# Unequal routing groups, shorter one-hot tiles, softmax by tanh and an earlier turn in a fused RNN and MoE kernel

## The chip, the cores and the metric

The kernel runs on one core of a Trainium2 chip. The metric is the device time of one execution in microseconds (us), the median over several executions. In this text PE is the matrix engine (TensorE), PEld its weight loads, DVE the vector engine, ACT the scalar engine, POOL the GpSimd engine and SP the engine that issues most DMAs. L721 is line 721 of the kernel before.

## What is computed

```python
# x (2, 1024, 256) as rows of 16 tokens; h0 = cond_1024 (2, 256)
step:   h = tanh(x_t @ Wx + b + h_prev @ Wh)          # a recurrence over 1024 tokens, two sequences
logits = h @ gate_w.T                                  # 8 experts
top_v, top_i = top_k(logits, 2)
probs  = softmax(top_v)
out    = x + sum over the two chosen experts e of
             probs_e * ((silu(h @ wg_e.T) * (h @ wu_e.T)) @ wd_e.T)   # 256 -> 1024 -> 256
```

The 2048 tokens form 16 tiles of 128. A step of the kernel's recurrence computes one tile: all 64 chunks of both sequences advance at once, and steps 48 to 63 give the tiles 0 to 15 of h that are used.

## The kernel before

**Stages.** Steps 8 to 63 of the recurrence (loop at L616, matmuls L623, tanh on ACT) come first. Routing lies among steps 49 to 63 and the first expert steps. Then the experts: the 2048 x 2 choices are sorted by expert into slots of 128 tokens; the tokens of a slot are gathered from DRAM (`rows_d`), turned into columns (`transpose_tokens`, L203), multiplied, and added to the output with an indirect DMA (`scatter`, L467). All matmuls of the experts split their operands into a high and a low part (`xhi`, `xlo`; `hh`, `hl`) and add three products.

**Routing.** Tiles are handled in groups of four (`GRP`, L36; `groups`, L341). For each tile `route_tile` (L350) transposes the tile and computes its logits on PE (L357), and ACT copies the row of 264 (256 of h, 8 logits) into the group's `rows`. `route_max` finds the two largest logits on DVE. For a group, `route_choice` makes one-hot choices `oh`, their sum `sel` and the difference `dl` of the two logits; `route_exp` takes exp(dl) on ACT; `route_position` (L388) counts on PE, by matmuls with `sel`, at which place of its expert each token stands, in `pos_ps`; `route_code` (L401) turns that into a slot number `v` and a place `m` in it, and, by `route_rows` (L446), the softmax weights, which POOL puts into `rows`; `rows_out` writes `rows` to DRAM in three DMAs on SP. `route_onehot` (L425) makes three tiles of 128 x 1024 f16 on DVE for a group: a one-hot of `v` (part 0, tile `bv`), its product with the token number (part 1), a one-hot of `m` (part 2, tile `am`). `route_slots` (L440) multiplies them on PE (L444) into `inv_ps`: for every place and slot the token that stands there.

**Early and late.** After two groups `early_slots` (L473) gathers two slots of expert 0 (POOL, L461), which hold only tokens of the first eight tiles; `early_turn` (L484) transposes them. This is unit 0. After the last group `all_slots` (L487) computes the index `gidx` and gathers the other two slots of expert 0 (unit 1). SP also writes a row `landed` that waits for the early gather (L480); what SP issues next waits behind it. `expert_order` (L496) then sorts the experts by load, in five parts.

**Order.** It is written out by hand, and every engine keeps it. `at(step, f)` (L548) notes a call under a number, `run(step)` (L551) makes all calls noted up to that number, in order of the numbers. In the recurrence `run(s - 0.5)` stands between the two halves of step s, `run(s)` behind it. An expert step n has `front` (L830: 12 matmuls of gate and up), `gate` (L849: Silu on ACT, product `g` on DVE, cast `hh` on ACT, difference on DVE) and `back` (L868: the down product) of an earlier step, with `run(64 + n + ...)` between them (L946 to L980). Unit 0's gates of steps 0 and 1 both come in step 1 (`shut`), and its `back` lags behind by two steps from step 5 on.

**Tables.** ACT holds one set of function tables at a time. Tanh and exp are in the one loaded at the start; another is loaded for Silu ahead of unit 0 (L592).

`route_max`, `route_choice`, `rows_out`, the gathers and scatters, and the split of the next expert's weights (`piece`, L766) are as before apart from their place. DVE, ACT and POOL instructions go through a helper and all have L54 in the profile, so they are told apart by their tiles.

Of the kernel before, what the change touches and what calls it, by code (L numbers as in the profile page):

```python
# [8 lines left out]
F32 = mybir.dt.float32  # L9
# [26 lines left out]
GRP = 4  # L36
# [21 lines left out]
def rnn_moe(ctx, tc, xT, xrows, h0T, Wx, Wh, b, gw, W, out):  # L58
# [21 lines left out]
    iota16 = cst.tile([P, P], F16, name="iota16")  # L80
    trash = cst.tile([P, E * SPE // MT, MT], F32, name="trash").rearrange("p a b -> p (a b)")
# [11 lines left out]
    def constants(part):  # L93
        if part == 0:
            vec.tensor_copy(iota_f, iota_i)
            vec.tensor_copy(tokp1, part_i)
            vec.tensor_scalar(ident, iota_f, 1.0, tokp1[:, 0:1], ALU.add, ALU.is_equal)
        elif part == 1:
            vec.tensor_scalar(upper, iota_f, 1.0, tokp1[:, 0:1], ALU.add, ALU.is_gt)
            vec.tensor_copy(ig[:, 0, 0:P], ident)  # L100
            vec.tensor_copy(ig[:, 1, E : P + E], ident)
            vec.tensor_copy(iota16, iota_f)
            vec.tensor_copy(tok16, tokp1.unsqueeze(2).to_broadcast([P, R, 2]))
        elif part == 2:
            vec.tensor_copy(trash, trash_i.rearrange("p a b -> p (a b)"))
            vec.memset(ones16, 1.0)
            vec.tensor_scalar(base, iota_f[:, 0:E], float(SPE), None, ALU.mult)
        else:

            vec.tensor_scalar(keyc, iota_f[:, 0:E], FIRST - 0.5, 2.0**17, ALU.is_lt, ALU.mult)  # L110
            vec.scalar_tensor_tensor(keyc, iota_f[:, 0:E], float(8 * P * SPE + 1), keyc, ALU.mult, ALU.add)
# [110 lines left out]
    rows2 = ov.tile([P, GRP * ROW], F32, name="rows2")  # L222
# [15 lines left out]
    act.activation(warm, zl[:, 0:1], AF.Tanh)  # L238
# [27 lines left out]
    pos_ps = y_tile(0)[:, 0 : (GRP + 1) * E].rearrange("p (i e) -> p i e", e=E)  # L266
# [75 lines left out]
    for g in range(R // GRP):  # L342
        o = (g % 2) * 4 * GRP * P
        gr = {"r0": g * GRP, "n": GRP}
        space = rows2 if g == 2 else xs[g % 3 % 2][:, 0 : GRP * ROW]
        gr["rows"] = space.rearrange("p (i c) -> p i c", c=ROW)
        gr["am"], gr["bv"] = (hot_space[:, o + c * 2 * GRP * P : o + (c + 1) * 2 * GRP * P].rearrange("p (i m) -> p i m", m=P) for c in range(2))
        groups.append(gr)
# [35 lines left out]
    def route_exp(gr):  # L384
        gr["ex"] = rt.tile([P, gr["n"]], F32, name="ex")
        act.activation(gr["ex"], gr["dl"], AF.Exp)

    def route_position(gr):  # L388

        n, r0 = gr["n"], gr["r0"]  # L390
        w = n + 1
        ops = [(ones16, base.unsqueeze(1).to_broadcast([P, w, E]), pos_ps), (upper, sel[:, r0 : r0 + n, :], pos_ps[:, 0:n, :])]
        for r in range(r0 + n):
            m = max(0, r - r0 + 1)
            ops.append((ones16, sel[:, r : r + 1, :].to_broadcast([P, w - m, E]), pos_ps[:, m:w, :]))
        for m, (l, x, o) in enumerate(ops):
            pe(nc.tensor.matmul(
                o.rearrange("p i e -> p (i e)"), lhsT=l, rhs=x,
                start=(m == 0), stop=(m == len(ops) - 1), skip_group_check=True))

    def route_code(gr):  # L401
        n = gr["n"]
        rows = route_rows(gr)
        tmp = rt.tile([P, n, 2, E], F32, name="tmp")
        next(rows)
        vec.tensor_tensor(tmp, gr["oh"], pos_ps[:, 0:n, :].unsqueeze(2).to_broadcast([P, n, 2, E]), ALU.mult)
        code = rt.tile([P, n, 2], F32, name="code")
        next(rows)
        vec.tensor_reduce(code, tmp, AX.X, ALU.add)
        next(rows, None)  # L410
        big = 1.5 * 2.0**23 * P
        vv = rt.tile([P, n, 2], F32, name="vv")
        vec.tensor_scalar(vv, code, 0.5 - P / 2, big, ALU.add, ALU.add)
        gr["v"] = v = rt.tile([P, 2 * n, 2], F16, name="v")
        twice = lambda t: t.rearrange("p i c -> p (i c)").unsqueeze(2).to_broadcast([P, 2 * n, 2])
        vec.tensor_scalar(v, twice(vv), -big, 1.0 / P, ALU.add, ALU.mult)
        gr["m"] = m = rt.tile([P, 2 * n, 2], F16, name="m")
        vec.scalar_tensor_tensor(m, v, -float(P), twice(code), ALU.mult, ALU.add)

    def early_gap():  # L420

        vec.tensor_scalar(gap, pos_ps[:, GRP, 0:1], -1.0 / P, float(ET), ALU.mult, ALU.add)
        vec.tensor_scalar(base[:, 0:1], gap, 0.0, None, ALU.max)

    def route_onehot(gr, part):  # L425


        n = gr["n"]
        sh = [P, 2 * n, P // 2, 2]
        pairs = lambda t: t.rearrange("p i (m t) -> p i m t", t=2)  # L430
        if part == 1:
            bv = gr["bv"].rearrange("p (i c) (m t) -> p i (c m) t", c=2, t=2)
            tok = tok16[:, gr["r0"] : gr["r0"] + n, :].unsqueeze(2).to_broadcast([P, n, P, 2])
            vec.tensor_tensor(bv, bv, tok, ALU.mult)
            return
        hot, x = ((gr["bv"], gr["v"]), None, (gr["am"], gr["m"]))[part]
        count = iota16.rearrange("p (m t) -> p m t", t=2).unsqueeze(1).to_broadcast(sh)
        vec.tensor_tensor(pairs(hot), count, x.unsqueeze(2).to_broadcast(sh), ALU.is_equal)

    def route_slots(gr, i):  # L440
        for c in range(2):
            first = gr["r0"] + i == 0 and c == 0
            last = gr["r0"] + i == R - 1 and c == 1
            pe(nc.tensor.matmul(inv_ps, lhsT=gr["am"][:, 2 * i + c, :], rhs=gr["bv"][:, 2 * i + c, :], start=first, stop=last, skip_group_check=True))  # L444

    def route_rows(gr):  # L446
        n, ex = gr["n"], gr["ex"]
        sm = rt.tile([P, n], F32, name="sm")
        vec.tensor_scalar(sm, ex, 1.0, None, ALU.add)
        yield  # L450
        pr = rt.tile([P, n, 2], F32, name="pr")
        vec.reciprocal(pr[:, :, 0], sm)
        yield
        vec.tensor_tensor(pr[:, :, 1], ex, pr[:, :, 0], ALU.mult)
# [32 lines left out]
    def all_slots():  # L487
# [4 lines left out]
        vec.scalar_tensor_tensor(key, pos_ps[:, GRP, :], 8.0, keyc, ALU.mult, ALU.subtract)  # L492
        vec.scalar_tensor_tensor(cnt, iota_f[:, 0:E], -float(P * SPE), pos_ps[:, GRP, :], ALU.mult, ALU.add)
# [72 lines left out]
    maxima.update({5: 55, 9: 59.5, 10: 60.6, 11: 61, 12: 62.2, 13: 62.3, 14: 64.05, 15: 64.06})  # L566
    for g, gr in enumerate(groups):
        for r in range(gr["r0"], gr["r0"] + gr["n"]):
            at(r + 49, route_tile, gr, r)
            at(maxima[r], route_max, gr, r)  # L570

    def group(g, choice, exp, position, code, hot, slots):
        gr = groups[g]
        at(choice, route_choice, gr)
        at(exp, route_exp, gr)
        at(choice + 0.1, rows_out, gr, ((0, P), (P + E, ROW)))
# [8 lines left out]
    group(0, 52.5, 52.6, 53.5, 53.5, (54, 54, 55), 56.5)  # L585
    group(1, 56.5, 56.6, 57.5, 57.5, (58, 58, 58), 60.1)
    at(58.1, early_gap)
    at(60.2, early_slots)
    group(2, 61, 61.1, 62, 62, (62.4, 64.1, 64.1), 65.12)
    at(63.5, early_turn)  # L590
    group(3, 64.07, 64.08, 65.1, 65.13, (65.2, 65.3, 66.3), 68.55)
    at(64.09, act.activation, warm, zl[:, 0:1], AF.Silu)  # L592
    at(68.55, all_slots)
    at(70.6, chunk_starts)
# [117 lines left out]
    with ExitStack() as c2:  # L712
# [66 lines left out]
        class Unit:  # L779
# [50 lines left out]
            def front(u, s):  # L830

                w, x = u.job.w, u.x
                if u.main:
# [8 lines left out]
                    pg, pu = (products(ab, p) for ab, p in zip(pairs, pt))  # L842
# [84 lines left out]
        def shut(n):  # L927

            u, s, j, m = step_of(n)
            low = []  # L930
            if (j, m) in split_at:
                to, p = split_at.pop((j, m))
                u.gate(s, lambda: low.append(jobs[to].piece(p, jobs[to + 1] if to + 1 < len(jobs) else None)))
            else:
                u.gate(s)
            for f in low:
                f()

        def step_of(n):
            i, s = steps[n]  # L940
            u = units[i]
            return u, s, jobs.index(u.job), s + (NIC if i and units[i - 1].job is u.job else 0)

        run(64)
        run(64.1)
        for n in range(len(steps)):  # L946
            i, s = steps[n]
            u = units[i]
            u.front(s)

            run(64 + n + 0.15)
            if n == 1:
                shut(0)
            run(64 + n + 0.2)
            if n > 0:
                shut(n)
# [7 lines left out]
            if n == 5:  # L964
                units[1].gather()
                units[2].gather()
            if i > 0 and s == 5 and i + 1 < len(units):
                units[i + 1].turn()
            for _ in range({6: 1, 7: 1, 9: 2, 11: 1}.get(n, 0)):
                next(order_ops)  # L970
            if i > 0 and s == (3 if i == 1 else 2) and i + 2 < len(units):
                units[i + 2].gather()
            if n < len(steps) - NIC + TAIL + 2:

                for late in {2: (), 3: (0,), 4: (1, 2)}.get(n, (n - 2,) if n > 4 else ()):
                    v, t = steps[late]
                    units[v].back(t)
            if n == 6:
                units[1].turn()
# [184 lines left out]
```

## Time and profile before

| | us |
|---|---|
| Median of 8 runs | 389.32 |
| Lowest and highest | 387.83, 389.66 |
| The profiled execution's own time | 389.44 |
| Its span (first to last instruction) | 387.3 |
| Steps 8 to 63 of the recurrence | to 75.3 |
| First gate matmul of unit 0 | 77.77 |
| Late gather: index, first matmul behind it | 90.55, 95.28 |
| End of PE's work | 371.9 |

A row of a timeline gives the start and the duration in us, engine, line, operation, output and inputs with their shape, the number of instructions merged, and in brackets the idle time of the engine before it and the instruction that ended it. Matmuls overlap, so that a single one looks longer than the distance to the next. In the chain of waits every step leads to what released it; its shares tell on which engine the time was spent that set the end. In a table by stages each row has the stretch, its length, busy time of PE, PEld, DVE, ACT and POOL with the number of instructions, the clock granted to PE (1.00 is full), the busy share of the DMA engines and GB/s. At its end the kernel spends some 15 us on the last scatters, from 371.9 on.

### The profile page before, as it was taken

The numbers are of one execution on the slowest core, as the hardware profiler recorded it, in microseconds if no ns is written. First come the engines' busy times: TensorE is split into PE (matmuls) and PEld (weight loads), VectorE is DVE, ScalarE is ACT, GpSimd is POOL, SyncE is SP. The second block draws the span as 40 slices with busy tenths as digits, with TensorE's granted clock in tenths as the row PEclk, the third lists the DMA queues.
The fourth block names the chain that finished last, engine by engine and source line by source line (L and its number), as shares of the span: only waits on it lengthen the run. The fifth ranks groups of instructions, "written<-read, shape, count | busy, mean of one in ns | idle before, by whom it ended". The sixth has DMA issues, their size and how long they took to land.

```text
span 387.3 us, 7243 instructions
## 1 busy us (share of the span) xinstructions
PE 370.6 (96%) x2715; PEld 350.5 (90%) x2715; DVE 227.0 (59%) x568; ACT 198.9 (51%) x460; POOL 117.7 (30%) x124
## 2 busy tenths in 40 slices
PE   8999999998999999999999999999999999999990
PEld 7998899897998889999999999999989999999890
DVE  6876648776678656574556564566545655663410
ACT  3746667543455644655446644665454555444420
POOL 3780001204264500674223602523040014006042
PEclk9999999999899999999999999999999999999996
DMA  7962334141166534665136243445143144003122
GB/s 216 414 256 96 108 111 113 31 113 46 41 162 192 154 110 136 151 195 112 68 123 130 67 130 91 85 136 137 27 111 114 47 171 53 0 2 40 12 23 35
DMA packets 19227, 42.20 MB, mean 109 GB/s; under 512 B 4802, under 2 KB 14178, under 8 KB 16066
## 3 DMA queue, kind: packets, MB, share of 16 engines
q1 hardware_dynamic: 12402, 32.32, 24.6%
q0 software_dynamic: 6496, 9.09, 14.7%
q8 instruction: 23, 0.38, 0.4%
q10 hardware_dynamic: 288, 0.26, 0.3%
q14 instruction: 18, 0.15, 0.1%
HBM read 35.15 MB, written 9.14 MB: 114 GB/s over the span
## 4 chain that ended last, share of the span: by engine, by line
PE 78%; DVE 8%; ACT 5%; POOL 3%; issue 3%; DMA 1%; POOLq 0%; DVEq 0%; ACTq 0%
PE pgu_t L721 42%; PE yb L883 21%; PE pgu_t L623 8%; PE ptr L303 2%; PE ptr L210 2%; POOL out_dram L468 2%; ACT hh L54 2%; DMA xg<-rows_d,gidx 1%; DVE wd L54 1%; DVE g L54 1%; DVE hh L54 1%; PE ptr L634 1%; ACT h L54 1%; ACT gu_g L54 1%; PE ptr L883 1%
## 5 line engine op out<-in xcount | busy, mean ns | idle before, releaser
L883 PE MATMUL yb<-wd,hh 128*128 128x256 f32 (+2 forms) x544 | 94.2, 284 | 0.2 <-ACT y L54 0.2
L54 DVE TENSOR_TENSOR g<-g,pgu_t 128x256 f32<-128x256 f32 (+5 forms) x96 | 50.1, 522 | 61.5 <-PE pgu_t L721 46.2
L883 PEld LDWEIGHTS yb<-wd,hh 128*128 128x128 f32 (+2 forms) x544 | 80.5, 185 | 2.3 <-ACT y L54 0.7
L468 POOL DMA_INDIRECT out_dram<-y,si x27 | 43.5, 1612 | 118.5 <-ACT y L54 113.0
L54 ACT CAST hh<-g 128x256 fp32r<-128x256 f32 (+5 forms) x92 | 44.6, 485 | 68.0 <-DVE g L54 67.2
L721 PE MATMUL pgu_t<-xhi,gu_g 128*128 128x256 f32 (+5 forms) x384 | 78.7, 327 | 0.3 <-ACT xhi L54 0.3
L54 ACT ACTIVATE g<-pgu_t 128x256 f32<-128x256 f32 (+5 forms) x96 | 44.8, 466 | 65.9 <-PE pgu_t L721 65.0
L721 PE MATMUL pgu_t<-xhi,gu_u 128*128 128x256 f32 (+5 forms) x384 | 78.1, 325 | 0.0
L721 PEld LDWEIGHTS pgu_t<-xhi,gu_u 128*128 128x128 f32 x384 | 61.6, 189 | 4.3
L721 PEld LDWEIGHTS pgu_t<-xhi,gu_g 128*128 128x128 f32 x384 | 59.2, 190 | 2.8 <-issue 0.5
L54 DVE TENSOR_TENSOR hl<-g,hh 128x480 fp32r<-128x480 f32 (+4 forms) x52 | 31.0, 597 | 31.8 <-ACT hh L54 31.8
L883 PE MATMUL yb<-wd,hl 128*128 128x256 f32 (+1 forms) x176 | 49.6, 282 | 0.0
L721 PE MATMUL pgu_t<-xlo,gu_u 128*128 128x256 f32 (+5 forms) x192 | 46.7, 325 | 0.0
L721 PE MATMUL pgu_t<-xlo,gu_g 128*128 128x256 f32 (+5 forms) x192 | 46.7, 324 | 0.0
L461 POOL DMA_INDIRECT xg<-rows_d,gi x27 | 30.6, 1135 | 50.7 <-DVE cm L812 19.7
L721 PEld LDWEIGHTS pgu_t<-xlo,gu_g 128*128 128x128 f32 x192 | 32.7, 189 | 2.3
L721 PEld LDWEIGHTS pgu_t<-xlo,gu_u 128*128 128x128 f32 x192 | 32.7, 189 | 2.2
L883 PEld LDWEIGHTS yb<-wd,hl 128*128 128x128 f32 (+1 forms) x176 | 32.2, 183 | 0.1
L623 PE MATMUL pgu_t<-h,wh 128*128 128x128 f32 (+1 forms) x224 | 28.6, 266 | 1.4
L54 DVE TENSOR_TENSOR hh<-g,hh 128x256 fp32r<-128x256 f32 x40 | 17.1, 427 | 21.7 <-ACT hh L54 21.7
L54 ACT ACTIVATE h<-pgu_t 128x128 f32<-128x128 f32 (+1 forms) x72 | 17.6, 276 | 13.7 <-PE pgu_t L623 9.0
L623 PEld LDWEIGHTS pgu_t<-h,wh 128*128 128x128 f32 x152 | 18.4, 190 | 4.2 <-ACT h L54 3.3
(166 smaller groups left out, 462.2 us busy)
## 6 DMA issues: line engine op xcount, KB each, us to landing
raw<-in_W_dram SPq DMA_DIRECT2D x24, 1024.0 KB, 5.0
gu_u<-in_xT_dram SPq DMA_DIRECT2D x6, 256.0 KB, 5.0
rows_d<-gu_u SPq DMA_DIRECT2D x6, 256.0 KB, 3.0
out_dram<-in_xrows_dram SPq DMA_DIRECT2D x1, 512.0 KB, 15.8
rows_d<-rows SPq DMA_DIRECT2D x2, 256.0 KB, 2.8
xg<-rows_d,gi POOLq DMA_INDIRECT x27, 3.1
out_dram<-y,si POOLq DMA_INDIRECT x27, 3.9
gu_u<-in_xT_dram ACTq DMA_DIRECT2D x2, 128.0 KB, 3.7
```

The source lines that it names most:

```text
L54: return lambda *a, **k: self.tc.keep_in_program_order(f(*a, **k))
L210: pe(nc.tensor.transpose(pt[:, m, j, :], tiles[i][:, k * (P + E) : k * (P + E) + P], ident))
L303: pe(nc.tensor.matmul(pt, lhsT=l, rhs=r, start=(i == 0), stop=(i == len(ops) - 1)))
L461: nc.gpsimd.indirect_dma_start(out=xg, out_offset=None, in_=rows[:, :], in_offset=bass.IndirectOffsetOnAxis(ap=idx, axis=0),)
L468: return nc.gpsimd.indirect_dma_start(out=out[:, :], out_offset=bass.IndirectOffsetOnAxis(ap=idx, axis=0), in_=y, in_offset=None, compute_ ...
L623: pe(nc.tensor.matmul(acc[s % 2][j], lhsT=w[:, k, j * P : (j + 1) * P], rhs=prev[k], start=False, stop=True, skip_group_check=True))
L634: pe(nc.tensor.matmul(pt, lhsT=zl, rhs=zl, start=True, stop=True))
L721: pe(nc.tensor.matmul(pt, lhsT=a[i], rhs=b[j], start=(i + j + n == 0), stop=(j == 1 and n == len(lhs_rhs) - 1), skip_group_check=True))
L883: pe(nc.tensor.matmul(yt[0:w, :], lhsT=h[a][:, i * P : i * P + w], rhs=wd[b][:, ic, :], start=(ic == 0 and first and n == 0), stop=(ic == ...
```

## The change

Groups have 5, 3, 5 and 3 tiles. After g groups a slot number within an expert is at most `reach` (6, 8, 14, 16), since so many tiles cannot fill more slots; `bv` holds only these columns (8 times `reach` for each one-hot, for 8 experts), compared with a `count` tile of that width, three of which are made at the start. `route_slots` writes into as many columns of each expert. The softmax of two values becomes 0.5 -/+ 0.5 tanh(dl / 2), and the one table loaded is Silu's. `rows2` is dropped: groups 0 and 2 share one space, groups 1 and 3 lie in the other one. The numbers in the order change, tile 15's `route_tile` moves between gate and up of expert step 0, `front` gets a place for that, `gate` n comes in step n, one-hots stand between `g` and `hh`, `back` lags by two steps from the start, and unit 1's `turn` stands ahead of the `back` of step 6.

```diff
-GRP = 4
+GROUPS = (5, 3, 5, 3)
...
+    reach = [-(-sum(GROUPS[: g + 1]) // 2) * 2 for g in range(len(GROUPS))]
+    count16 = [iota16 if n == SPE else cst.tile([P, E * n], F16, name=f"count{n}") for n in reach]
...
+            for n, t in zip(reach, count16):
+                if n < SPE:
+                    vec.tensor_copy(t.rearrange("p (e j) -> p e j", e=E), iota_f.rearrange("p (e j) -> p e j", e=E)[:, :, 0:n])
...
-    rows2 = ov.tile([P, GRP * ROW], F32, name="rows2")
...
-    act.activation(warm, zl[:, 0:1], AF.Tanh)
+    act.activation(warm, zl[:, 0:1], AF.Silu)
...
-    for g in range(R // GRP):
-        o = (g % 2) * 4 * GRP * P
-        gr = {"r0": g * GRP, "n": GRP}
-        space = rows2 if g == 2 else xs[g % 3 % 2][:, 0 : GRP * ROW]
-        gr["rows"] = space.rearrange("p (i c) -> p i c", c=ROW)
-        gr["am"], gr["bv"] = (hot_space[:, o + c * 2 * GRP * P : o + (c + 1) * 2 * GRP * P].rearrange("p (i m) -> p i m", m=P) for c in range(2))
+    for g, n in enumerate(GROUPS):
+        r0 = sum(GROUPS[:g])
+        gr = {"r0": r0, "n": n, "count": count16[g], "reach": reach[g]}
+        o = r0 // NA * GROUPS[1] * ROW if g % 2 else 0
+        gr["rows"] = xs[g % 2][:, o : o + n * ROW].rearrange("p (i c) -> p i c", c=ROW)
+        o = g % 2 * 2 * GROUPS[2] * (P + E * reach[2])
+        gr["am"] = hot_space[:, o : o + 2 * n * P].rearrange("p (i m) -> p i m", m=P)
+        o += 2 * n * P
+        gr["bv"] = hot_space[:, o : o + 2 * n * E * reach[g]].rearrange("p (i m) -> p i m", m=E * reach[g])
...
-        act.activation(gr["ex"], gr["dl"], AF.Exp)
+        act.activation(gr["th"], gr["dl"], AF.Tanh, scale=0.5)
...
-        count = iota16.rearrange("p (m t) -> p m t", t=2).unsqueeze(1).to_broadcast(sh)
-        vec.tensor_tensor(pairs(hot), count, x.unsqueeze(2).to_broadcast(sh), ALU.is_equal)
+        hot, x, count = ((gr["bv"], gr["v"], gr["count"]), None, (gr["am"], gr["m"], iota16))[part]
+        sh = [P, 2 * n, count.shape[1] // 2, 2]
+        count = count.rearrange("p (m t) -> p m t", t=2).unsqueeze(1).to_broadcast(sh)
+        vec.tensor_tensor(hot.rearrange("p i (m t) -> p i m t", t=2), count, x.unsqueeze(2).to_broadcast(sh), ALU.is_equal)
...
-            pe(nc.tensor.matmul(inv_ps, lhsT=gr["am"][:, 2 * i + c, :], rhs=gr["bv"][:, 2 * i + c, :], ...))
+            to = inv_ps.rearrange("p (e j) -> p e j", e=E)[:, :, 0 : gr["reach"]]
+            bv = gr["bv"][:, 2 * i + c, :].rearrange("p (e j) -> p e j", e=E)
+            pe(nc.tensor.matmul(to, lhsT=gr["am"][:, 2 * i + c, :], rhs=bv, ...))
...
-        vec.tensor_scalar(sm, ex, 1.0, None, ALU.add)
-        vec.reciprocal(pr[:, :, 0], sm)
-        vec.tensor_tensor(pr[:, :, 1], ex, pr[:, :, 0], ALU.mult)
+        vec.tensor_scalar(pr[:, :, 0], th, -0.5, 0.5, ALU.mult, ALU.add)
+        vec.tensor_scalar(pr[:, :, 1], th, 0.5, 0.5, ALU.mult, ALU.add)
...
-    maxima.update({5: 55, 9: 59.5, 10: 60.6, 11: 61, 12: 62.2, 13: 62.3, 14: 64.05, 15: 64.06})
+    maxima.update({5: 55, 8: 58.2, 9: 59.2, 10: 60.3, 11: 61, 13: 62.3, 14: 63.2, 15: 64.13})
...
-            at(r + 49, route_tile, gr, r)
+            at(r + 49 if r < 15 else 64.1, route_tile, gr, r)
...
-    def group(g, choice, exp, position, code, hot, slots):
+    def group(g, choice, weight, position, code, hot, slots):
...
-    group(0, 52.5, 52.6, 53.5, 53.5, (54, 54, 55), 56.5)
-    group(1, 56.5, 56.6, 57.5, 57.5, (58, 58, 58), 60.1)
-    at(58.1, early_gap)
-    at(60.2, early_slots)
-    group(2, 61, 61.1, 62, 62, (62.4, 64.1, 64.1), 65.12)
-    at(63.5, early_turn)
-    group(3, 64.07, 64.08, 65.1, 65.13, (65.2, 65.3, 66.3), 68.55)
-    at(64.09, act.activation, warm, zl[:, 0:1], AF.Silu)
-    at(68.55, all_slots)
-    at(70.6, chunk_starts)
+    group(0, 53.5, 53.6, 54.5, 54.5, (54.6, 54.6, 55.1), 57.1)
+    group(1, 56.5, 56.6, 57, 57, (57.1, 57.1, 57.1), 59)
+    at(57.6, early_gap)
+    at(59, early_slots)
+    group(2, 61.5, 61.6, 62, 62, (62.4, 63.3, 64.2), 66.6)
+    at(62.1, early_turn)
+    group(3, 64.13, 64.14, 65.1, 65.13, (65.2, 66.2, 67.2), 67.6)
+    at(67.6, all_slots)
+    at(69.6, chunk_starts)
...
-                    pg, pu = (products(ab, p) for ab, p in zip(pairs, pt))
+                    pg = products(pairs[0], pt[0])
+                    between()
+                    pu = products(pairs[1], pt[1])
...
-            u.front(s)
-
+            u.front(s, lambda: run(64 + n + 0.1))
             run(64 + n + 0.15)
-            if n == 1:
-                shut(0)
-            run(64 + n + 0.2)
-            if n > 0:
-                shut(n)
+            low = []
+
+            def beside():
+                run(64 + n + 0.2)
...
+            u.gate(s, beside)
...
-            if n == 5:
+            if n == 4:
                 units[1].gather()
                 units[2].gather()
-            if i > 0 and s == 5 and i + 1 < len(units):
+            if s == (6 if i == 0 else 5) and i + 1 < len(units):
                 units[i + 1].turn()
-            for _ in range({6: 1, 7: 1, 9: 2, 11: 1}.get(n, 0)):
+            for _ in range({5: 1, 6: 1, 7: 2, 9: 1}.get(n, 0)):
                 next(order_ops)
-            if i > 0 and s == (3 if i == 1 else 2) and i + 2 < len(units):
+            if i > 0 and s == 2 and i + 2 < len(units):
                 units[i + 2].gather()
-                for late in {2: (), 3: (0,), 4: (1, 2)}.get(n, (n - 2,) if n > 4 else ()):
-                    v, t = steps[late]
-                    units[v].back(t)
-            if n == 6:
-                units[1].turn()
+            if 2 <= n < len(steps) - NIC + TAIL + 2:
+                v, t = units[steps[n - 2][0]], steps[n - 2][1]
+                v.back(t)
```

## The prediction

> **What bounds the kernel now.** I read the page, then the chain of waits, then the timeline of each engine from 52 to 132 us. TensorE (PE) is busy nearly throughout, and the chain is mostly its matmuls:
>
> ```profile
> span 387.3 us, 7243 instructions
> PE 370.6 (96%) x2715; PEld 350.5 (90%) x2715; DVE 227.0 (59%) x568; ACT 198.9 (51%) x460; POOL 117.7 (30%) x124
> PE 78%; DVE 8%; ACT 5%; POOL 3%; issue 3%; DMA 1%; POOLq 0%; DVEq 0%; ACTq 0%
> ```
>
> So an edit is worth what it takes from PE's own work, or from the few places where PE waits. The change touches 52 to 97 us only (and three small copies at the start); behind that PE runs on to 372 us with one wait of note (0.25 us at 127.4). PE's waits, in its timeline (start, busy, then the idle before it and what ended it):
>
> ```profile
> 64.04 0.62 PE L444 MATMUL yb<-wd 128*128 128x128 f16 x8 [0.16 <-DVE wd L54]
> ...
> 70.50 0.68 PE L623 MATMUL pgu_t<-gu_g,wh 128*128 128x128 f32 x4 [0.47 <-ACT rows L54]
> ...
> 76.45 0.55 PE L210 MATMUL pgu_t<-ident,xg 128*128 128x128 f32 x3 [0.43 <-DMA xg<-rows_d,gidx]
> ...
> 77.77 0.71 PE L721 MATMUL pgu_t<-xhi,gu_g 128*128 128x256 f32 x4 [0.30 <-ACT xhi L54]
> ...
> 93.85 0.33 PE L210 MATMUL ptr<-ident,xg 128*128 128x128 f32 x1 [0.69 <-DMA xg<-rows_d,gidx]
> 95.28 0.55 PE L210 MATMUL ptr<-ident,xg 128*128 128x128 f32 x3 [1.10 <-DMA xg<-rows_d,gidx]
> ```
>
> The bracket counts from a modelled end that lies some 0.2 behind PE's pace. Measured against the pace (a recurrence step 0.89, a routing tile 0.47, twelve 128x256 matmuls 1.41, six 0.71) these starts are late by 0.38, 0.62, 0.58, 0.46, 0.85 and 1.31: **4.20 us**. The last two are the late gather. A table by stages (PE busy after the first sum, granted clock behind the last bracket) shows what follows them:
>
> ```profile
> 93.00:96.40 3.40, 1.61 (x13) 1.26 (x12) 1.39 (x5) 0.94 (x2) 2.48 (x4) 1.00 0.35 98
> 96.40:99.90 3.50, 3.50 (x20) 3.50 (x18) 2.21 (x7) 0.83 (x3) 1.76 (x2) 0.51 0.43 118
> ```
>
> Clock 0.51 for about 3.4 us: matmuls that take 0.47 and 0.71 elsewhere take 0.76 and 1.28 there. Against the pace the 18 matmuls from 96.37 lose **1.52 us**.
>
> Why is the gather late? Its index (gidx) comes out of DVE:
>
> ```profile
> 83.48 0.43 DVE L54 TENSOR_TENSOR hh<-g,hh 128x256 fp32r<-128x256 f32 x1 [0.47 <-ACT hh L54]
> 83.83 0.68 DVE L54 TENSOR_TENSOR wd<-iota,v 128x1024 f16<-128x1024 f16 x1
> 84.43 0.42 DVE L54 TENSOR_TENSOR g<-g,pgu_t 128x256 f32<-128x256 f32 x1
> 85.32 0.42 DVE L54 TENSOR_TENSOR hh<-g,hh 128x256 fp32r<-128x256 f32 x1 [0.47 <-ACT hh L54]
> ...
> 90.55 0.17 DVE L54 TENSOR_SCALAR gidx<-yb 128x18 int32<-128x18 f32 x1
> ```
>
> A round (g, wait for ScalarE's cast, hh, a one-hot) takes 1.83 us, 0.47 of it waiting, and five rounds stand before gidx. The second gathered tile lands 4.68 us after gidx starts (95.23).
>
> **The change, part by part.**
>
> One-hots. 128x1024 f16 takes 0.68, as 128x512 f32 does (0.69; 128x256 f32: 0.42), so an f16 element costs half of (0.69-0.42)/256 = 0.53 ns. To the next start it is 0.60, or 0.72 if that needs the result. Twelve of 1024 become 480, 480, 1280; 384, 384, 768; 1120, 1120, 1280; 3 x 768: 9600 elements for 12288, 1.4 us less of DVE. By length: 384 0.26, 480 0.31, 768 0.46, 1120 0.65, 1280 0.73.
>
> Slot matmuls (L444). Eight with 128 columns pace 0.45 (0.055 each); L397's f16 matmuls with 40 columns run at 0.40/16 = 0.025. Ten of 48, six of 64, ten of 112 and six of 128 columns I take at 0.030, 0.035, 0.050, 0.055: 1.34 for 1.80. Gain **0.45** (bounds 0 and 0.6), less 0.05 for two more L397 matmuls.
>
> Softmax. Three DVE ops become two, but the reciprocal and the product stand between dependent ops: code starts 0.25 behind tmp and vv 0.25 behind code with or without them. Gain 0 to 0.2 per group; I take 0. Tanh in Silu's table: Tanh takes 0.28 for 128x128 and a copy 0.27, so I take no change. The built order has one table load for two. The load removed (1.28 at 79.92) ended at 81.20, while Silu's first reader on DVE (g, 82.60) stood behind the code of group 3: 0 now, but left in the new order it would cost up to 1.3. The Trainium skill (ScalarE: Activation LUTs, What ACT_TABLE_LOAD costs) puts a switch at 1.28 plus a drain of 1.38; ScalarE was busy with exp until 79.90 and the load started at 79.92, so the trace shows no such drain; with it the switch would have ended at 82.58, just ahead of 82.60, and the sum stays.
>
> Start. Three copies (128x128 f32 to f16 takes 0.22) stand on DVE before a wait of 1.51 for wx at 4.82: 0. Without that cover, 0.4.
>
> rows2 goes, so tile 8's ScalarE copy now waits for group 0's three DMAs. Its last one was issued at 61.47 with packets to 63.1; a step later and 5/4 as long it lands by about 64.7, and the copy is due at 65.9. 0; beyond that ScalarE, its tanh and PE slip one for one. The expert-order steps come one or two steps sooner and unit 3's gathers one: in steps 7 to 9 DVE then has 2.1 of g and hh, 2.2 of these and a split of 1.1 against PE's 3 x 2.13, so 0; without that room 0.5. On SP, group 2's rows stay behind the write that waits for the early gather, and move forward with it; group 3's last DMA lands near 84, before the late gather starts.
>
> The order. I wrote the changed order down from the built programs and laid it out by these intervals from 58.9 us on; f32 work behind an f16 burst gets 0.08 (59.52 to 60.04 holds 0.44 of work).
>
> - Group 1. DVE's code for group 0 ends at 62.16 (a step later). Then two seeds 0.38, the three one-hots 1.50 with the wait for the first, two maxima 0.70: group 1's choice starts its maximum at 64.74 and writes sel at 65.65 (65.36 before). PE reaches the positions at 64.6, since they moved up from mid-step 58 and the slots of group 0, with their wait, moved behind them. **New wait 1.05.** Behind it on PE stand all of step 58 and its tanh.
> - Then group 1's one-hots are 1.1 for 1.9: the seed for step 61 is in time (0.62 gone). gidx for the early gather starts at 69.4 (71.67), its second tile lands at 74.1 (76.41), and PE gets to the transposes at 74.6: 0.58 gone. They now stand in the middle of step 63, whose second half and tile 14 (0.91) cover the cast xhi: 0.46 gone.
> - Group 2's positions stand half a step nearer to their sel: tile 12's copy, maximum, oh, sel take 1.56 from tile 12's end and PE has 1.36 of work: **new wait 0.2**. xlo: **0.1**.
> - Group 3's positions come behind gate matmuls of step 1; sel has to wait for xlo 0.60, two one-hots of 1120, three maxima, ready at 79.3; PE is there at 78.65: **new wait 0.7**. Before, front 1 and these positions ended at 81.33; now front 1 at 80.6.
> - The one-hots now stand between g and hh, where DVE waited 0.47 for the cast. A round is 0.34 + 0.46 + 0.34 = 1.14, and four rounds precede gidx, not five. But slots of group 3 come one step sooner and wait for the last one-hot (86.1) from 85.4: **new wait 0.8**. gidx at 86.65, second tile 4.68 later, 91.35. PE has 5.65 of work behind the slots and transposes at 92.25. So 0.85 + 1.31 go, cover left 0.9, and with them the half clock, 1.52.
>
> Sum by terms: 4.20 + 1.52 + 0.40 - (1.05 + 0.2 + 0.1 + 0.7 + 0.8) = 3.3. By the layout unit 1's first step, which ended at 100.72, ends at 97.0: 3.7. I take 3.5. The profiled execution took 389.44 (span 387.3); the median of the runs shown is 389.32. **Forecast 385.9 us.**
>
> The clock. The dip followed a stretch with 1.6 of 3.4 us busy and no gap above 1.31. The recurrence around 30 to 50 us keeps 1.00 though PE idles 0.3 in every 1.19. So an idle share of a quarter is safe and one of a half is not; my waits reach 1.05 in 3.4. The Trainium skill (TensorE: Matmul & The Clock Gate, Part 1) wants a whole idle window of about 3.4 us before the clock halves; the trace needed less. By the page neither old nor new waits would bring a dip; the dip of before is measured, so the sum keeps it.
>
> **Rivals.**
>
> *The DVE chain stays long* (0.20). If g, cast and hh do not interleave as laid out and a round keeps 1.83, three rounds cost 2.1 more; the slots of group 3 then wait 2.9 and the late gather loses its cover only in part, PE being late as well: 385.9 + 2.1 = 388.0; with half of it 387. For it: hh waits for a ScalarE that also does Silu. Against: ScalarE is idle over 1 us before four of those five casts.
>
> *The new waits cost the clock* (0.10). A wait that leaves PE half idle in a window costs 1.5: 387.4, twice 388.9, which is no change.
>
> *Slower* (0.07): the shorter one-hots lose the double rate. They then run at 1.06 ns an element, as 128x1024 f32 does (1.22). That puts 1.2, 0.8, 1.8 and 1.2 us on DVE in the four groups: group 1's wait becomes 2.2, group 3's 1.9, its slots' 2.6 or more, and the late gather (cover 0.9) waits again with a dip. Losses 1.2 + 1.2 + 1.8 + 1.5 + about 1 = 6.7 against 3.5: 392.5. It decides at the 128x480 one-hot: 0.40 or 0.65. Against it: the pairs of equal values on the innermost axis are kept. The Trainium skill (VectorE: DVE Perf Modes, What auto-detection actually checks) asks for 16-bit tensors with step 1, which the new tiles are; by that rule this rival falls.
>
> *No step as said* (0.03): Tanh not in Silu's table would put loads of 1.28 on each switch, over 395; the built order speaks against it.
>
> *The forecast* has 0.60: 384 to 387.
>
> **The numbers.** The range takes in new waits of half the size with slots at their lower bound (3.5 + 1.4 + 0.15, 384.4; less the 0.4 by which terms and layout differ) and the long chain: 384.0 to 388.0. A change of 0.2% (0.8 us) is about what a measurement of this kernel tells from none: faster than 388.5 is the forecast, the long chain and most of the clock's: 0.83; within, 0.08; slower 0.09.
>
> **What would show it.** L444's six or ten matmuls at 0.2 to 0.5 in all; a wait of PE near 1 us before group 1's positions (L397's successor) with DVE sel behind it; the early transposes and the gate matmuls behind them without a wait; no wait for xg at the late transposes and clock 1.00 behind them; gidx about 4 us sooner. Wrong if PE still waits for xg there, if a window at half clock appears elsewhere, or if 128x480 takes 0.6.

## The result, and the profile after

The changed kernel takes **385.81 us** (median of 17 runs, 385.38 to 386.50), the kernel before 388.95 (median of 46, 387.38 to 389.97): ratio 0.9925, 95% interval 0.9914 to 0.9936. Forecast were 385.9 in 384.0 to 388.0. By the two medians the gain is 3.1 us; the 3.5 of the forecast was subtracted from a median of eight runs, 389.32, which lay 0.4 above that of all 46. The profiled execution has a span of 384.1 for 387.3. The page of the changed kernel, its lines on the span, on PE and on the chain of waits:

```profile
span 384.1 us, 7245 instructions
PE 368.4 (96%) x2717; PEld 349.0 (91%) x2717; DVE 226.3 (59%) x567; ACT 197.9 (52%) x458; POOL 116.4 (30%) x124
PE 90%; DVE 2%; POOL 2%; ACT 1%; DMA 1%; issue 1%; POOLq 0%; DVEq 0%; ACTq 0%
```

PE is the bound still; the share of the chain that passed through DVE and ACT went from 13% to 3%. PE's timeline, the rows in which it waited, and the late transposes:

```profile
65.41 0.17 PE L408 MATMUL yb<-sel,upper 128*128 128x24 f16 x1 [0.90 <-DVE sel L54]
...
75.50 0.55 PE L216 MATMUL pgu_t<-ident,xg 128*128 128x128 f32 x3 [0.95 <-DMA xg<-rows_d,gidx]
...
80.31 0.17 PE L408 MATMUL yb<-sel,upper 128*128 128x24 f16 x1 [0.47 <-DVE sel L54]
...
87.24 0.51 PE L455 MATMUL yb<-wd 128*128 128x128 f16 x6 [0.74 <-DVE wd L54]
...
93.28 0.60 PE L216 MATMUL ptr<-ident,xg 128*128 128x128 f32 x4
```

By the same paces as in the prediction these rows are late by 1.04, 1.13, 0.62 and 0.91; group 2's positions add 0.27 and xlo 0.17: **4.14 us of waits, for 4.20 before**. The waits were exchanged, not removed. The last row has no bracket: all four late transposes run in one piece. The table by stages for the two stretches shown of before:

```profile
93.00:96.40 3.40, 3.40 (x31) 3.40 (x30) 2.76 (x11) 1.56 (x4) 2.00 (x3) 1.00 0.34 96
96.40:99.90 3.50, 3.50 (x32) 3.50 (x32) 2.89 (x10) 1.83 (x4) 0.00 (x0) 1.00 0.11 35
```

PE is busy throughout and the clock is 1.00 where it was 0.51.

One row of the table of before needs a correction: 371.9 is where the last piece of PE on the chain of waits begins, not where PE ends. PE's last row ended at 377.6; the scatters from 373.1 on run beside it. The same piece begins at 368.7 now, 3.2 sooner.

### The profile page after: what moved, and what is told of

Read it like the earlier page. It is cut to its first block, busy times and chain, and to the rows that moved or that the text cites. A ratio compares the mean times of both kernels' runs of the same rounds, so it can differ in the third digit from the quotient of the medians.

```text
span 384.1 us, 7245 instructions
## 1 busy us (share of the span) xinstructions
PE 368.4 (96%) x2717; PEld 349.0 (91%) x2717; DVE 226.3 (59%) x567; ACT 197.9 (52%) x458; POOL 116.4 (30%) x124
## 4 chain that ended last, share of the span: by engine, by line
PE 90%; DVE 2%; POOL 2%; ACT 1%; DMA 1%; issue 1%; POOLq 0%; DVEq 0%; ACTq 0%
PE pgu_t L728 48%; PE yb L892 23%; PE pgu_t L630 9%; PE ptr L309 3%; PE ptr L216 2%; POOL out_dram L476 2%; PE pgu_t L892 1%; DMA xg<-rows_d,gidx 1%; PE pgu_t L284 1%; PE ptr L367 1%; PE ptr L641 1%; DVE wd L54 1%; ACT h L54 1%; PE ptr L294 1%; PE ptr L892 1%
## 5 line engine op out<-in xcount | busy, mean ns | idle before, releaser
L469 POOL DMA_INDIRECT xg<-rows_d,gi x27 | 29.2, 1083 | 48.7 <-DVE cm L819 19.7
```

Source lines behind the costliest of these rows:

```text
L469: nc.gpsimd.indirect_dma_start(out=xg, out_offset=None, in_=rows[:, :], in_offset=bass.IndirectOffsetOnAxis(ap=idx, axis=0),)
```

## The experiments

The runs form three groups, each on one chip beside the kernel before. The changed kernel itself ran beside them in the third group alone; in the other two, its 385.81 stands for it. Single executions are not compared as a whole: the first routing tile starts at 52.4 to 53.0 in most traces, but at 53.4 to 53.9 in three (wide tiles, one-hots, the chain of copies) that have no more work ahead of it. So local losses are taken from PE's timeline, between the same matmuls of two kernels.

**Is the late gather, with the clock behind it, what was repaired?** A chain of copies delays it:

```diff
+        src = gidx[:, ET:n]
+        for d in range(12):
+            to = slack[d % 2][:, 0 : n - ET]
+            pool.tensor_copy(to, src)
+            src = to
-        late_tiles.extend(gather(gidx[:, i : i + 1]) for i in range(ET, MT))
+        late_tiles.extend(gather(src[:, i - ET : i - ET + 1]) for i in range(ET, MT))
```

> The changed kernel with a chain of twelve dependent copies of the index on POOL ahead of the late gather, which delays that gather, and it alone, by 3 to 4 us (in the earlier attempt the twelve copies were placed between the gathers and the second tile came only 0.02 later). Theory A: the cover is 0.95 us, so PE waits 2 to 3 us at the late transposes, and a window at half clock follows in some or most executions (1.5 us): slower by 2 to 4.5 us than the changed kernel. Rival B (a later gather is hidden, the change gained elsewhere): under 1 us.

Measured: 390.04 (388.19 to 391.45), beside 385.37 for the changed kernel on that chip: +4.7. PE's timeline of this kernel, then its table by stages for one window of the clock record and the next:

```profile
95.90 0.30 PE L217 MATMUL ptr<-ident,xg 128*128 128x128 f32 x1 [1.64 <-DMA xg<-rows_d,slack]
97.05 0.55 PE L217 MATMUL ptr<-ident,xg 128*128 128x128 f32 x3 [0.85 <-DMA xg<-rows_d,slack]
```

```profile
94.81:98.22 3.41, 1.47 (x11) 1.31 (x12) 0.95 (x3) 0.99 (x2) 2.50 (x4) 1.00 0.35 102
98.22:101.64 3.42, 3.42 (x18) 3.42 (x18) 1.48 (x5) 0.38 (x2) 1.61 (x2) 0.50 0.44 121
```

The waits cost 2.90 against the pace, the 3.41 us at half clock 1.53: 4.43 in this execution. (It took 6.2 more than the changed kernel's profiled one; 1.7 of the rest stood ahead of unit 0's first matmul, where the edit does nothing.) Theory A holds, the median a little above its range. The mean clock tells the executions apart: nine at 0.986 to 0.989 took 389.8 to 391.5, two at 0.992 and 0.993 took 388.2 and 388.8. The kernel before splits in the same way: on the first chip 14 executions at 0.989 or less have a median of 389.15, nine at 0.992 or more 387.83; on the second 389.86 (12) and 388.59 (18); on the third 389.79 (11) and 387.61 (5). At 0.990 stand times of both kinds. The changed kernel's are at 0.990 or more, and its times do not split. So the change gained the clock in some four to six of ten executions, and some 2 us beside it.

An earlier attempt, with twelve independent copies written ahead of the gathers, says nothing: they were placed between the gathers, and the second tile was issued 0.02 later.

```diff
+        for _ in range(12):
+            pool.tensor_copy(slack, inv)
```

> The changed kernel with twelve copies of 128x128 on POOL behind gidx and ahead of the late gather, which delay this gather by some 3.5 us and nothing else (POOL has no other work there). Theory A (the late gather is what the change repaired: its tile lands 0.95 us ahead of PE, and a wait there costs itself and then half the clock for 3.4 us): PE waits about 2.5 us in all at the late transposes, in most executions a window at half clock follows (1.5 us): slower by 3.5 to 4.5 us than the changed kernel, 2.5 where the clock stays. Rival B (a later gather is hidden by other work, and the change gained elsewhere): under 1 us.

Measured: 387.44 (386.36 to 388.10), without any wait at the late transposes; its loss of 1.2 us lies behind unit 1's first front (last section). The expectation was missed, since the gather was not delayed.

**The other way round: the kernel before with the gather given more cover.**

```diff
-            if n == 6:
+            if n == 7:
                 units[1].turn()
```

> The kernel before with one edit: unit 1's transposes of the late gather one expert step later, behind the back of the step 7, so that a front and a back (2.1 us) cover the gather. Theory A (the late gather and the clock behind it are most of what the change gained): the waits of 0.85 and 1.31 and the half clock (1.5, in about two of three executions of the kernel before by their mean clock) go, and a wait of about 1.0 for the casts of xhi and xlo comes, which nothing covers now: faster by 1.2 where the clock was whole before, by 2.7 where not; 386.2 to 386.8 in the median, with a narrow spread. Rival B (the gain came from the shorter one-hots and the slot matmuls): 0.3 us or less, and the half clock stays.

Measured: 388.45 (387.86 to 391.02), ratio 0.999, interval 0.9968 to 1.0012: inconclusive as a time, and short of the 386.2 to 386.8 expected. Its PE timeline shows what the edit did:

```profile
94.90 0.72 PE L210 MATMUL ptr<-ident,xg 128*128 128x128 f32 x4
96.45 0.73 PE L721 MATMUL pgu_t<-xhi,gu_g 128*128 128x256 f32 x4 [0.83 <-ACT hh L54]
97.58 0.50 PE L721 MATMUL pgu_t<-xlo,gu_g 128*128 128x256 f32 x2 [0.39 <-DVE eid_i L54]
```

In this execution the gather's waits and the half clock are gone; the casts cost 1.95 in their place (1.0 expected: an expert-order step stands ahead of xlo on DVE). Of the other eleven executions two have a clock of 0.989 or less (390.24 and 391.02). Unit 1's first front ended at 98.62 for 100.72; 0.6 of these 2.1 were lost again at a wait for ACT's y at 125.9 (0.79, for 0.25 before), and 0.6 at another at 176.6 (0.31, for none before). So what the gather and the clock cost is shown, but as a time this edit alone does not win it.

**The shorter one-hots.**

```diff
-    reach = [-(-sum(GROUPS[: g + 1]) // 2) * 2 for g in range(len(GROUPS))]
+    reach = [SPE for g in range(len(GROUPS))]
```

> The changed kernel with every one-hot as wide as before (128 columns for each; groups of 1280, 768, 1280, 768 elements in all three parts), all else the same. Theory A (DVE's chain sets PE's waits): two one-hots of group 0 take 0.73 for 0.31 and hold group 1's choice 0.84 us longer, so the wait of 1.04 at group 1's positions becomes about 1.9; group 1's own two cost 0.4 more, which the early gather shows in part; the slot matmuls take 0.5 us more: slower by 1.3 to 2.0 us than the changed kernel (387.1 to 387.8). Rival B (DVE is busy 59% of the span and one-hots lie off the path): only the slot matmuls show, 0.4 to 0.6 us (386.3).

Measured: 388.20 (386.67 to 389.31); five executions at a clock of 0.992 or more have a median of 387.4, six at 0.989 or less 388.9, so by the mean clock the wide tiles bring the half clock back in half of them. In the profiled execution (clock whole) PE waited 1.9 at group 1's positions, for 1.04:

```profile
66.95 0.17 PE L408 MATMUL yb<-sel,upper 128*128 128x24 f16 x1 [1.73 <-DVE sel L54]
```

Unit 1's first front ended 1.57 later than in the changed kernel, but 0.70 of that stood ahead of the first routing tile already, and 0.9 is left; the wait at the early transposes was 0.6 shorter here. Theory A by its wait and by the executions with the whole clock (1.6 more than 385.81); the median, 2.4 more, lies above its range. So the two short tiles of groups 0 to 2 carry between a quarter and three quarters of the gain of 3.1, depending on the clock and on the measure.

**One table.** The softmax by exp, and with it the load for Silu, put back:

```diff
-        act.activation(gr["th"], gr["dl"], AF.Tanh, scale=0.5)
+        act.activation(gr["th"], gr["dl"], AF.Exp)
...
+    at(64.145, act.activation, warm, zl[:, 0:1], AF.Silu)
```

> The changed kernel with the softmax of before (exp, sum, reciprocal, product) and so with two tables: Tanh and Exp first, and a table load for Silu behind group 3's exp. Theory A: group 3's exp stands at about 80.4, directly ahead of the first Silu (80.48), so the load of 1.28 us delays that Silu, g and the one-hots behind it; slots of group 3 come 0.6 to 1.3 us later and PE waits so much longer: slower by 0.6 to 1.3 us than the changed kernel. Rival B (the load is hidden, as it was in the kernel before, and the softmax operations stand between dependent ones): within 0.2 us.

Measured: 388.56 (387.86 to 389.09), +2.75, over twice the most that theory A allows. ACT's timeline shows the first part:

```profile
79.95 0.20 ACT L54 ACTIVATE th<-dl 128x3 f32<-128x3 f32 x1 [1.54 <-DVE dl L54]
80.16 1.28 ACT L54 ACT_TABLE_LOAD   x1
81.46 0.20 ACT L54 ACTIVATE warm<-zl 128x1 f32<-128x1 f32 x1
81.57 0.37 ACT L54 ACTIVATE g<-pgu_t 128x256 f32<-128x256 f32 x1
```

The load stands between group 3's exp and the first Silu (80.48 in the changed kernel). From PE's first front to the end of unit 1's first this cost 1.13. The other 1.4 came behind it, in 270 us without a wait: PE's matmuls were slower. The extra tile of the softmax takes 64 bytes (two buffers of 32), and the tiles behind it moved by as much. So the next run moves them and does nothing else:

```diff
+    pad = rt.tile([P, 8], F32, name="pad")
+    pool.memset(pad, 0.0)
```

> The changed kernel with one unused tile of 64 bytes (two buffers of 32) ahead of the x tiles, so that xhi, xlo and the later small tiles lie 64 bytes further on, exactly where they lie in the run with two tables. In that run PE's matmuls of the expert steps ran 0.7% slower through most of the kernel (a 128x480 matmul 381 ns for 378), 1.4 us in all behind unit 1's first front. Theory A (the address of the moving operand does that): slower by 1.2 to 1.6 us than the changed kernel, with 381 ns. Rival B (it came with the second table or with that run): within 0.2 us.

Measured: 387.48 (387.09 to 388.96), +2.1 on the changed kernel of that chip. The groups by form, one row of the changed kernel and the same row of the moved one:

```profile
L728 PE MATMUL pgu_t<-xlo,gu_g 128*128 128x480 f32 x48 | 14.2, 378 | 0.0
```

```profile
L730 PE MATMUL pgu_t<-xlo,gu_g 128*128 128x480 f32 x48 | 14.4, 381 | 0.0
```

Behind unit 1's first front it lost 1.4 us, stretch by stretch within 0.03 of the run with two tables, and 0.2 in the fronts ahead of it: 1.6, theory A. The other 0.5 of the difference stood ahead of the first front of unit 0, 0.4 of it ahead of the first routing tile. For the table itself 2.75 - 2.1 = 0.65 is left, by PE's timeline 1.1.

**One-hots between g and hh.**

```diff
-            def beside():
-                run(64 + n + 0.2)
+            run(64 + n + 0.2)
+
+            def beside():
```

> The changed kernel with the one-hots of groups 2 and 3 in the expert steps ahead of g again, not between g and hh. Theory A (as the prediction's step has it, the interleaving shortens each of three rounds by the wait of 0.47 for the cast): slots of group 3 wait 1.0 to 1.4 us longer, and the time rises by about that. Rival B (in the changed kernel's trace the third one-hot stands behind a g that waits until 86.30 for ScalarE and PE; ahead of that g it would not wait, which gives back what the rounds lose): slots within 0.3 us of now, the time within 0.3 us.

Measured: 386.53 (385.46 to 386.80), interval of the ratio 0.9924 to 0.9966; between PE's first front and unit 1's +0.07. As a time it is 0.72 above 385.81, more than rival B allows, but 0.67 of that stands ahead of the first routing tile in the trace, where the edit does nothing. Rival B by the mechanism: a round is longer by 0.47 as the step said (1.70 from g to g), but the third one-hot no longer waits for g, and PE waits for it as long as in the changed kernel (0.74 there in the bracket):

```profile
87.79 0.51 PE L455 MATMUL yb<-wd 128*128 128x128 f16 x6 [0.76 <-DVE wd L54]
```

**Why does the early gather still hold PE?** The changed kernel's DMA view from 72.4 to 75.4 (40 slices of 0.075; then the queues):

```profile
DMA  0000599914891100000000030000030000000000
...
q0 software_dynamic: 48, 0.14, 17.3%
q8 instruction: 1, 0.02, 2.0%
```

The gather's packets begin in slices 5 to 14, and then one each in slices 24 and 30. The trace's packets: the q8 packet, 16384 bytes, lies at 73.26 to 74.20; the gather's last two at 74.19 to 74.64 and 74.63 to 74.99; all others had landed by 73.55. Eight more traces (the changed kernel again, the first of the reordered one, both runs with late copies, and those on table, wide tiles, one-hots and shift) have the same picture: the gather's last two packets begin within 0.02 us of the fetch's end and land one behind the other. Two runs move the fetch against the gather, by more instructions on PE ahead of it (32 and 64 more rows in the profile):

```diff
-                pe(nc.tensor.matmul(acc[a][j], lhsT=zl, rhs=zl, start=True, stop=True, skip_group_check=True))
+                for c in range(2):
+                    o = slice(c * 64, (c + 1) * 64)
+                    pe(nc.tensor.matmul(acc[a][j][:, o], lhsT=zl, rhs=zl[:, o], start=True, stop=True, skip_group_check=True))
```

> The changed kernel with the eight zero matmuls at its start cut in halves of 64 columns: the same work, 32 more instructions (loads and matmuls) on PE ahead of everything else. Theory A (a code fetch holds the early gather): in the changed kernel's trace a packet of 16384 B of the queue q8 instruction lies at 73.26 to 74.20, and the last two 4224 B packets of the second gathered tile land only behind it (74.64, 74.99), 1.45 us after the others (73.55). PE runs some 18 instructions per us there, so the fetch comes about 1.8 us sooner (71.5), the second tile lands whole near 73.6 to 73.9, PE's wait of 1.13 us at the early transposes goes, and the time falls by 0.8 to 1.2 us against the changed kernel (about 384.8 against 385.81). Rival B (the gather itself takes longer now, for its rows are written later and in groups of five): the fetch moves, the last packets still come near 75.0, the wait stays at 1.1 and the time within 0.2 us.

```diff
+        if 30 <= s < 46:
+            pe(nc.tensor.matmul(ptr_tile()[:, 0:8], lhsT=zl, rhs=zl[:, 0:8], start=True, stop=True))
```

> The changed kernel with one tiny extra matmul (zeros, 128x8, result unused) in each of the steps 30 to 45, behind the step's own matmuls, where PE waits 0.3 us per step for the tanh anyway: 64 more PE instructions (loads and matmuls), hidden. Theory A (the code fetch holds the early gather): in the run with the start cut in halves the same 64 instructions brought the fetch 3 us nearer and PE's wait at the early transposes was gone, but the start cost 3.3 to 3.8. Here the start costs nothing: the fetch ends before the second gathered tile's packets come, the wait of 1.13 goes, the time falls by 0.8 to 1.2 us against the changed kernel (384.6 to 385.0 where that has 385.8). Rival B (the wait went in that run for another reason, as the late start): wait and time stay.

Measured: 388.82 (388.19 to 389.43) and 388.94 (388.29 to 389.56). As times both expectations failed. The start in halves cost 3.8 (the smaller matmuls take as long as the larger ones), the fillers some 1.1 (not hidden). In the run with the fillers PE's first front came as in the changed kernel (0.04 later), and 3.2 us were lost behind it (last section). The mechanism held in both: the fetch came 3 us sooner against the early transposes (4.1 us ahead of them, for 1.0), and the wait was gone. The second run's early transposes, in one piece:

```profile
75.49 0.60 PE L216 MATMUL pgu_t<-ident,xg 128*128 128x128 f32 x4
```

The Trainium skill (Runtime: NRT & Kernel Launch, Instruction fetch mechanics) has each engine refill its instructions in blocks of 16 KiB, 256 instructions, through a DMA queue of its own, and calls the cost mostly hidden; the packet size agrees, the shift only roughly, for 32 and 64 more rows moved it alike; the cost here is a wait of PE of 1.13 us for another queue's packets (0.58 in another execution of the changed kernel, where the fetch lay at 72.29 to 73.32).

**Do the new waits cost time, and is there a faster version?**

```diff
-    group(0, ..., (54.6, 54.6, 55.1), 57.1)
-    group(1, 56.5, 56.6, 57, 57, (57.1, 57.1, 57.1), 59)
+    group(0, ..., (54.6, 54.6, 55.1), 57)
+    group(1, 56.5, 56.6, 57.5, 57.5, (57.5, 57.5, 57.5), 59)
-    group(3, 64.13, 64.14, 65.1, 65.13, (65.2, 66.2, 67.2), 67.6)
+    group(3, 64.13, 64.14, 65.14, 65.145, (65.2, 66.2, 67.14), 67.6)
```

> The changed kernel with another order at the new waits: slots of group 0 ahead of group 1's positions, these between the halves of step 58; group 3's positions behind the whole front 1; group 3's third one-hot ahead of g of step 3. Theory A (the new waits of 1.04, 0.62 and 0.91 us are real time, for PE has nothing else in its queue): 0.25 + 0.44 of the first go, all of the second, and 0.4 to 0.8 of the third: faster by 1.0 to 1.7 us than the changed kernel. Rival B (the waits only move to the early transposes and to the slots of group 3, which hang on DVE and the gather): within 0.4 us.

Measured: 387.86 (387.04 to 389.18) on the second chip. PE reached unit 1's transposes 1.84 sooner, then lost 1.7 at unit 1's first front and 1.1 by 125. The expectation failed as a time. So it was run again, with the changed kernel beside it:

> The changed kernel once more, unaltered, on the same chip as the three that follow, for in the runs of the fetch by fillers, of the waits and of the late copies PE's signals to ScalarE came 1 to 3 us late in places (at 93 to 97 and at 111 to 118), which no run on the other chip shows. Theory A (that belongs to the chip or the moment): 385.4 to 386.5, all gates of the expert steps within 0.3 us of the end of their matmuls. Rival B (the kernel itself has it at times): some executions at 387 and more.

> The reordered kernel of the run on the waits, unaltered (slots of group 0 ahead of group 1's positions and these half a step later, group 3's positions behind front 1, its third one-hot ahead of g). There PE reached unit 1's transposes 1.84 us sooner than in the changed kernel, and lost 2.5 us to signals that came late. Theory A (the waits are real, the losses are the chip's): 383.8 to 384.6, faster than the changed kernel by 1.2 to 2.0 us. Rival B (what PE gains there it loses behind it, as DVE and ScalarE have no slack): within 0.5 us of the changed kernel.

Measured: the changed kernel 385.37 (385.21 to 385.56), the reordered one **384.35** (383.97 to 385.09), four runs each: faster by 1.0. The time lies in theory A's range, the difference is a little short of it. It is 0.9873 of the kernel before (0.9839 to 0.9907). It is the best version here. The rows of its PE from 55 us on that still have a bracket:

```profile
74.26 0.55 PE L216 MATMUL pgu_t<-ident,xg 128*128 128x128 f32 x3 [0.46 <-DMA xg<-rows_d,gidx]
85.16 0.51 PE L455 MATMUL yb<-wd 128*128 128x128 f16 x6 [0.52 <-DVE wd L54]
```

## Why the prediction was right, step by step

- **Late gather and clock: right.** gidx came at 87.79 (86.65 said), the second tile landed near 92.3, PE reached the transposes at 93.28: cover 0.95 (0.9 said). No wait, no half clock.
- **One-hots: right.** They kept the double rate. To the next start: 480 elements 0.32, 768 0.47, 1120 0.64, 1280 0.73 (0.31, 0.46, 0.65, 0.73 said); the duration at which the slower rival decided came out at 0.40. DVE's timeline:

```profile
62.10 0.40 DVE L54 TENSOR_TENSOR wd<-count,v 128x480 f16<-128x480 f16 x1
...
63.21 0.81 DVE L54 TENSOR_TENSOR wd<-iota,m 128x1280 f16<-128x1280 f16 x1
```

- **Slot matmuls: right.** 0.25, 0.18, 0.48 and 0.32 are 1.23, for 1.75 before: 0.52 (0.45 said).
- **Sum: right.** Up to unit 1's first front the terms give 0.06 for the waits, 0.52 for the slots and 1.52 for the clock, 2.1; the trace shows 2.46 without the start. The prediction's layout was 0.4 above its terms as well; where they lie stays open.
- **New waits: right.** 1.04, 0.27, 0.17, 0.62 and 0.91, for 1.05, 0.2, 0.1, 0.7 and 0.8. None brought the half clock. The prediction's bound between a quarter and a half of idle time set two measures side by side: its 0.3 in 1.19 goes by PE's pace, while the table's own count has PE busy for 18.71 of the 20 us from 30 on. The last section has both sides by one count.
- **Early gather: wrong.** "Its second tile lands at 74.1 and PE gets to the transposes at 74.6: 0.58 gone." gidx was in time (69.15), the tile landed only at 75.4, and PE waited 1.13. Everything up to unit 1's first front is later by that: its end at 97.99 (97.0 said), a gain of 2.7 in place of 3.7. The trace of before shows a like fetch at 72.68 to 73.97, over 1 us ahead of its second tile's last packets (to 76.1). The prediction moved the gather by over 2 us towards it and left it out.
- **What filled the gap.** 0.27 us came from the start of the execution, where the changed kernel's own two traces differ by 0.33, and the wait of 0.25 at 127.4 fell away. Without these the time would have been some 0.5 higher: the closeness to 385.9 is partly luck.
- **Interleaving: the reason was wrong, the sum not.** The layout had the third one-hot between g and hh; whether it stands there or ahead of g makes 0.07. So the rival of the long chain was priced too high too: rounds of 1.70 did not lengthen PE's wait.
- **Table: nothing, as said, but only against the old order.** There the load was hidden. In the new order it would stand on the path and cost 0.65 to 1.1, so this part lets the others work.

## What to carry to other kernels

When PE is the bound and its waits are short, ask first which wait brings a half clock behind it: here it cost half to two thirds as much as the waits ahead of it, and in total the waits stayed the same. The reordering mostly moved waits, so lay out the changed order and price each new one; half a step of other work between producer and consumer then took most of them (384.35). And an ablation that adds or drops a tile can move the tiles behind it: run the same shift by itself, or its time is not that of the part.

## What the runs showed of the hardware

- **Clock.** Records come in windows of 3.413 us or multiples (92.16 is 27 of them), and their phase against the kernel differs by execution: the first began 4.3 us into the span in the profiled execution before, 6.1 after. The windows ahead of the two seen at 0.50 had PE busy for 1.63 of 3.42 and 1.47 of 3.41. Counted on from the first record, no other whole window up to 370 us in the fourteen traces was under 2.15 (the run with wide tiles, 65.7 to 69.1), and each of these was followed by 1.00: the outcome changed somewhere between 1.63 and 2.15. A wait that falls across two windows leaves each busier. That this is why only some executions slow down is an inference. The Trainium skill (TensorE: Matmul & The Clock Gate, Part 1) asks for a whole idle window; here half of one was enough, and the measurement decides.
- **Addresses.** With xhi, xlo and the small tiles behind them 64 bytes further on in SBUF, most matmuls that read xhi or xlo took longer (128x480 of xlo 381 ns for 378, 128x256 of xlo 283 to 284 for 279 to 281 on that chip), while those of the down product stayed at 284, and the kernel lost 1.4 us; a few stretches became faster (21.31 us for 21.47 from 251.2 on). The runs with wide tiles and with late copies, which drop or add other tiles, kept 378. Why is open.
- **Late signals.** In three runs of the second group (the fillers, the reordered kernel, the independent copies) ACT started 1 to 3 us after the matmuls that, by the trace, it waited for had ended. In the run with the fillers a front ended at 93.3, and its Silu came at 95.50:

```profile
95.50 0.39 ACT L54 ACTIVATE g<-pgu_t 128x256 f32<-128x256 f32 x1 [2.75 <-PE ptr L216]
```

The reordered kernel lost 2.8 us so there, and nothing on the third chip. Its cause stays open.
